# A chunked recurrence in 256 chunks instead of 128, with its states added to the output by accumulating transfers

## The chip, the cores and the metric

The kernel runs on one core of a Trainium2 chip. A core has five engines with a queue of instructions each: TensorE (PE in the profile; PEld is its weight load), VectorE (DVE), ScalarE (ACT), GpSimd (POOL) and SyncE (SP, which here only starts transfers). [...] Sixteen DMA engines move data between the chip's memory (HBM) and the core's two memories: SBUF with 128 partitions, and PSUM, into which TensorE writes. The metric is the device time of one execution in microseconds (us), median of the runs.

## The reference, cut to what matters

The input x has the shape (4, 128, 64, 64): 4 batches, 128 channels, 4096 tokens each. Layer 0 is attention over all tokens of a batch with 64 channels, added to x. Layer 1 takes the tokens, adds causal attention of their normalized form, and then adds a recurrence:

```python
Wx = ((flat - mean) * jax.lax.rsqrt(var + BN_EPS) * gamma + beta).reshape(B, T, H)
def step(yt, wx_t):
    yt = jax.nn.sigmoid(wx_t + yt @ Vt)
    return (yt, yt)
```

`flat` is the normalized token times W, for all batches and tokens; mean and variance are taken over all 16384 rows. `step` runs over the 4096 tokens of a batch, from a state of zeros. The result is the attention result plus the states, for every token. All is float32. V is an orthogonal 128x128 matrix, and the slope of the sigmoid is at most 1/4, so two states that start apart come closer by a factor of four or more with each step.

## The kernel before, in words

The program is `fast_path`, followed by `general_path`, which runs only if `fast_path` has raised a flag. The flag says that a softmax sum left its range or that the cut recurrence did not meet its tolerance.

`fast_path` first does both attention layers, batch after batch, in blocks of 512 query tokens. A loop over items (pairs of key tiles) issues scores (lines 604 and 613), exponentials (618, 620), sums (644, 652) and values (664, 672), with the work of finished blocks slotted in between. The resident tensor `xs` holds x for all batches (64 KB per partition), channels on partitions, and is used over again: after layer 1, `finish1` sends a block's attention result, transposed back, to a scratch tensor `x2` in HBM (line 557), multiplies the normalized tokens by W (563), takes their statistics (564) and copies the product into `xs` (565). At the end of attention, `xs` thus holds Wx for all tokens, and `x2` the attention result.

The tail is the recurrence. It can't be run as 4096 steps in a row, so each batch is cut into `NCH` chunks of `STEPS` tokens, and all chunks of all batches step together: a step is a matmul with as many columns as there are chunks. Before, STEPS is 32 and NCH is 128; 4 batches make 512 columns, in two halves `g` of 256 columns that take turns.

- The attention result is loaded back into `xr` (line 750).
- The normalization's scale and shift are worked out from the statistics (753 to 761), with a square root on ScalarE.
- VectorE makes `wn`, the normalized Wx in step order, in 32 instructions (767).
- A first pass of 32 steps starts all chunks from nothing. Each step preloads `wn` into PSUM with a matmul by the identity (771), adds V times the previous states with a second matmul (782), and takes the sigmoid into SBUF (786). The states of the first 16 steps go to spare tiles, the last of them to `kept`; the later ones replace `wn`.
- The last state of each chunk, shifted by one chunk, is the start of the next (804). A second pass of 16 steps starts from it. Its last states are compared with `kept` (809 to 815): if they agree within 1e-6, the later 16 steps of the first pass stand.
- VectorE adds the states to `xr` in eight instructions, two per batch (833), and SyncE's queue stores the sum (836).
- The counts of both checks meet in `total` (824), one matmul (826) and the flag (827).

The tile library allocates tiles from pools, inserts the semaphore waits, and may move an instruction that is ready ahead of others; each engine's queue then runs in the order built. The helper `normed` has the reciprocal square root of the layer norm: GpSimd's power function (512) and a Newton step of four VectorE instructions (515 to 518).

Of the kernel before, what the change touches and what calls it, by code (L numbers as in the profile page):

```python
# [342 lines left out]
def fast_path(  # L343
# [26 lines left out]
    TPB = BLK // P  # L370
    SHIFT = 32.0
    LOW, HIGH = 1e-25, 1e25
    WARM, TOL, STEPS = 16, 1e-6, 32
    NCH = N // STEPS

    const = ctx.enter_context(tc.tile_pool(name="const", bufs=1))
    xpool = ctx.enter_context(tc.tile_pool(name="x", bufs=1))
    dram = ctx.enter_context(tc.tile_pool(name="dram", bufs=1, space=bass.MemoryType.DRAM))

    xs = xpool.tile([P, B, N], F32, name="xs")

    x2 = dram.tile([B, P, N], F32, name="x2")

    def load(name, shape, *parts):
        t = const.tile(shape, F32, name=name)
# [30 lines left out]
    g1 = const.tile([P, P], F32, name="g1")  # L418
    recs = const.tile([P, 2, B, NT], F32, name="recs")
    stats = const.tile([P, B * NB, nc.vector.BN_STATS_DIM], F32, name="stats")  # L420

    with tc.tile_pool(name="batch", bufs=1) as batch, tc.tile_pool(name="rows", bufs=2) as rowp, tc.tile_pool(
        name="prob", bufs=4
# [78 lines left out]
        def normed(b, g, dst):  # L502

            st = stat.tile([P, TPB, nc.vector.BN_STATS_DIM], F32, tag="st", name="ln_st")
            mv = stat.tile([P, TPB, nc.vector.BN_AGGR_DIM], F32, tag="mv", name="ln_mv")
            for j in range(TPB):
                nc.vector.bn_stats(st[:, j], xs[:, b, ds(g * BLK + j * P, P)])  # L507
                nc.vector.bn_aggr(mv[:, j], st[:, j])
            var = stat.tile([P, TPB], F32, tag="var", name="ln_var")
            nc.vector.tensor_scalar(var, mv[:, :, 1], LN_EPS, None, ALU.add)  # L510
            y = stat.tile([P, TPB], F32, tag="rstd", name="ln_rstd")
            nc.gpsimd.tensor_tensor(y, var, mhalf, ALU.pow)  # L512

            z = stat.tile([P, TPB], F32, tag="z", name="ln_z")
            nc.vector.tensor_tensor(z, y, y, ALU.mult)  # L515
            nc.vector.tensor_tensor(z, z, var, ALU.mult)
            nc.vector.tensor_scalar(z, z, -0.5, 1.5, ALU.mult, ALU.add)
            nc.vector.tensor_tensor(y, y, z, ALU.mult)
# [25 lines left out]
        def finish1(b, g):  # L544
            agg, den = bs[b].agg, bs[b].den
            mem = {}

            def first():
                project(1, b, g, agg, den)
                mem["xh"] = wk.tile([P, TPB, P], F32, tag="xh2", name="xh2")  # L550
                normed(b, g, mem["xh"])

            def second():
                t = xs[:, b, ts(g, BLK)].rearrange("p (j c) -> p j c", c=P)
                xc = wk.tile([P, BLK], F32, tag="xc", name="xc")
# [12 lines left out]
            yield 3, second  # L568
            yield 1, third
# [171 lines left out]

    GB = B // 2
    with tc.tile_pool(name="wn", bufs=1) as wnp, tc.tile_pool(name="y", bufs=2) as yp, tc.tile_pool(
        name="ps_y", bufs=3, space=PSUM
    ) as ps_y:
# [4 lines left out]
        mv = wnp.tile([P, nc.vector.BN_AGGR_DIM], F32, name="mv")  # L752
        nc.vector.bn_aggr(mv, stats)
        scale = wnp.tile([P, 1], F32, name="scale")
        nc.vector.tensor_scalar(scale, mv[:, 1:2], BN_EPS, None, ALU.add)
# [3 lines left out]
        shift = wnp.tile([P, 1], F32, name="shift")  # L759
# [4 lines left out]
        wn = wnp.tile([P, STEPS, B, NCH], F32, name="wn")  # L764
        by_step = xs.rearrange("p b (c s) -> p s b c", s=STEPS)
        for s in range(STEPS):
            nc.vector.tensor_scalar(wn[:, s], by_step[:, s], scale, shift, ALU.mult, ALU.add)

        def preload(s, g):
            ps = ps_y.tile([P, GB, NCH], F32, tag=f"y{g}", name=f"y{g}_ps")  # L770
            nc.tensor.matmul(ps, lhsT=ident, rhs=wn[:, s, ts(g, GB)], start=True, stop=False, skip_group_check=True)  # L771
            return ps

        def run(first, steps, place):

            prev = first
            nxt = [preload(steps[0], g) for g in range(2)]
            for s in steps:
                for g in range(2):
                    ps = nxt[g]  # L780
                    if prev[g] is not None:
                        nc.tensor.matmul(ps, lhsT=vf, rhs=prev[g], start=False, stop=True, skip_group_check=True)  # L782
                    if s != steps[-1]:
                        nxt[g] = preload(s + 1, g)
                    y = place(s, g)
                    nc.scalar.activation(y, ps, AF.Sigmoid)
                    prev[g] = y
            return prev

        kept = [wnp.tile([P, GB, NCH], F32, name=f"kept{g}") for g in range(2)]  # L790

        def place_first(s, g):
            if s == WARM - 1:
                return kept[g]
            if s < WARM:
                return yp.tile([P, GB, NCH], F32, tag=f"y{g}", name=f"y{g}")
            return wn[:, s, ts(g, GB)]

        last = run([None, None], range(STEPS), place_first)

        start = [wnp.tile([P, GB, NCH + 1], F32, name=f"start{g}") for g in range(2)]
        for g in range(2):
            nc.gpsimd.memset(start[g][:, :, 0:1], 0.0)
            nc.vector.tensor_copy(start[g][:, :, 1:], last[g])
        again = run([start[g][:, :, :NCH] for g in range(2)], range(WARM), lambda s, g: wn[:, s, ts(g, GB)])


        for g in range(2):
            nc.vector.tensor_tensor(kept[g], again[g], kept[g], ALU.subtract)
        count = wnp.tile([P, 3], F32, name="count")  # L810
        for g in range(2):
            k = kept[g].rearrange("p b c -> p (b c)")
            nc.vector.tensor_tensor(k, k, k, ALU.mult)
            nc.vector.tensor_scalar(k, k, TOL * TOL, None, ALU.is_le)
            nc.vector.tensor_reduce(count[:, g : g + 1], k, AX.X, ALU.add)

        r = recs.rearrange("p l b t -> p (l b t)")
        r2 = start[0].rearrange("p b c -> p (b c)")[:, : 2 * B * NT]
# [3 lines left out]
        nc.vector.tensor_reduce(count[:, 2:3], r, AX.X, ALU.add)  # L822
        total = wnp.tile([P, 1], F32, name="total")
# [3 lines left out]
        nc.vector.tensor_scalar(flag, tp, P * (B * NCH + 2 * B * NT) - 0.5, None, ALU.is_lt)  # L827

        for b in range(B):
            yb = wn[:, :, b, :]  # L830
            xb = xr[:, b, :].rearrange("p (c s) -> p s c", s=STEPS)
            for part in (slice(WARM, STEPS), slice(0, WARM)):
                nc.vector.tensor_tensor(xb[:, part], xb[:, part], yb[:, part], ALU.add)  # L833
# [61 lines left out]
```

## Time and profile before

The profile is of one execution; its span runs from the first to the last instruction on the core.

| what | value |
|---|---|
| median of 3 runs | 2282.46 us (2281.8 to 2282.84) |
| the profiled execution's own time | 2282.64 us |
| its span | 2280.9 us |
| TensorE matmuls, busy | 2221.0 us, 97% |
| VectorE busy | 1416.9 us, 62% |
| ScalarE busy | 1001.4 us, 44% |
| GpSimd busy | 104.7 us, 5% |
| moved by DMA | 36.17 MB |
| last matmul of attention (line 563) | starts at 2156.7 us |
| first matmul of the recurrence (line 771) | 2163.2 us |
| last sigmoid ends | 2250.6 us |

Positions in time are microseconds from the start of the span. A group's line names the source line, the engine and the operation, what it writes and reads, and the count; then busy time, mean time of one in nanoseconds, and the idle time of the engine before it with what ended it. A line of the timeline has start, duration, engine, line and operation, and in square brackets the idle time before. An instruction's duration contains some latency that the next on the same engine overlaps.

### The profile page before, as it was taken

The numbers are of one execution on the slowest core, as the hardware profiler recorded it, in microseconds if no ns is written. First come the engines' busy times: TensorE is split into PE (matmuls) and PEld (weight loads), VectorE is DVE, ScalarE is ACT, GpSimd is POOL, SyncE is SP. The second block draws the span as 40 slices with busy tenths as digits, with TensorE's granted clock in tenths as the row PEclk, the third lists the DMA queues.
The fourth block names the chain that finished last, engine by engine and source line by source line (L and its number), as shares of the span: only waits on it lengthen the run. The fifth ranks groups of instructions, "written<-read, shape, count | busy, mean of one in ns | idle before, by whom it ended". The sixth has DMA issues, their size and how long they took to land.

```text
span 2280.9 us, 31663 instructions
## 1 busy us (share of the span) xinstructions
PE 2221.0 (97%) x12928; PEld 1043.9 (46%) x12928; DVE 1416.9 (62%) x2607; ACT 1001.4 (44%) x1108; POOL 104.7 (5%) x207
## 2 busy tenths in 40 slices
PE   7999999999999999999999999999999999999894
PEld 3434355454333345544434445554434335554483
DVE  4877764444788764544687875454577786544435
ACT  3666623333566533333566642323466653333242
POOL 0000000000000000000000001000000001000000
PEclk9999999999999999999999999999999999999897
DMA  4000000000000000000000000000000000000123
GB/s 157 1 1 1 1 10 10 5 5 5 6 1 1 1 5 10 10 5 5 6 1 1 1 1 10 10 5 10 5 1 1 1 1 10 10 5 5 65 93 149
DMA packets 10536, 36.17 MB, mean 16 GB/s; under 512 B 1936, under 2 KB 2704, under 8 KB 8848
## 3 DMA queue, kind: packets, MB, share of 16 engines
q1 hardware_dynamic: 8640, 33.56, 3.8%
q8 instruction: 103, 1.69, 0.3%
q10 hardware_dynamic: 1744, 0.53, 0.1%
q14 instruction: 49, 0.40, 0.1%
HBM read 17.30 MB, written 16.78 MB: 15 GB/s over the span
## 4 chain that ended last, share of the span: by engine, by line
PE 95%; DVE 3%; issue 1%; DMA 0%; POOL 0%; ACT 0%; ACTq 0%; POOLq 0%; DVEq 0%
PE s_ps L613 20%; PE acc L672 20%; PE s_ps L604 20%; PE acc L664 19%; PE o_ps L493 3%; PE den_ps L488 2%; PE y_ps L771 2%; PE y_ps L782 2%; PE r_ps L465 1%; PE wx_ps L563 1%; PE v_ps L460 1%; PE r_ps L479 1%; DVE xr L833 1%; PE kc_ps L452 1%; PE xhT_ps L528 1%
## 5 line engine op out<-in xcount | busy, mean ns | idle before, releaser
L644 DVE TENSOR_TENSOR dsum<-dsum,p 128x1024 f32<-128x1024 f32 x676 | 827.7, 1224 | 507.7 <-ACT p L620 336.5
L618 ACT ACTIVATE p<-s_ps,nshift 128x1024 f32<-128x1024 f32 x512 | 571.4, 1116 | 379.7 <-PE s_ps L604 379.2
L620 ACT ACTIVATE p<-s_ps 128x1024 f32<-128x1024 f32 (+2 forms) x288 | 274.5, 953 | 632.4 <-PE s_ps L613 551.5
L604 PE MATMUL s_ps<-rows,kc 64*64 64x512 f32 x4096 | 538.4, 594 | 0.0
L664 PE MATMUL acc<-p,v 64*64 64x512 f32 x4096 | 535.0, 590 | 0.0
L613 PE MATMUL s_ps<-rows,xhT 128*128 128x512 f32 (+3 forms) x1152 | 504.8, 560 | 2.6 <-DVE rows L481 2.6
L672 PE MATMUL acc<-p,xh 128*128 128x512 f32 (+3 forms) x1152 | 501.5, 557 | 0.0
L672 PEld LDWEIGHTS acc<-p,xh 128*128 128x128 f32 x1152 | 215.8, 190 | 243.4 <-issue 234.9
L613 PEld LDWEIGHTS s_ps<-rows,xhT 128*128 128x128 f32 x1152 | 210.4, 190 | 229.1 <-issue 184.6
L664 PEld LDWEIGHTS acc<-p,v 64*64 64x64 f32 x4096 | 158.9, 133 | 279.9 <-issue 273.9
L604 PEld LDWEIGHTS s_ps<-rows,kc 64*64 64x64 f32 x4096 | 146.9, 133 | 248.3 <-issue 233.8
L512 POOL TENSOR_TENSOR ln_rstd<-ln_var,mhalf 128x4 f32<-128x4 f32 x64 | 66.7, 1042 | 1222.9 <-DVE ln_var L510 1212.1
L498 DVE SCALAR_TENSOR_TENSOR xs<-o_ps,recs,xs 128x128 f32<-128x128 f32 x256 | 72.9, 344 | 38.4 <-PE o_ps L493 38.4
L652 DVE TENSOR_TENSOR dsum<-dsum,p 128x256 f32<-128x256 f32 (+1 forms) x120 | 55.9, 496 | 64.3 <-POOL p L624 64.3
L488 PEld LDWEIGHTS den_ps<-ones,den 128*128 128x128 f32 x512 | 64.6, 191 | 40.5 <-issue 20.5
L642 DVE COPY dsum<-p 128x1024 f32<-128x1024 f32 x60 | 41.4, 690 | 61.7 <-ACT p L620 55.4
L520 DVE TENSOR_SCALAR xh<-xs,ln_mv,ln_rstd 128x128 f32<-128x128 f32 x256 | 71.2, 341 | 1.9
L624 POOL TENSOR_SCALAR_AFFINE_SELECT p<-p 128x128 f32<-128x128 f32 x128 | 34.5, 293 | 743.1 <-ACT p L620 743.1
L488 PE MATMUL den_ps<-ones,den 128*128 128x1 f32 x512 | 63.9, 246 | 0.0
L771 PE MATMUL y_ps<-wn,ident 128*128 128x256 f32 x192 | 58.4, 393 | 5.5 <-issue 5.5
L507 DVE BATCH_NORM_STATS2 ln_st<-xs 128x6 f32<-128x128 f32 x256 | 63.4, 269 | 0.0
L515 DVE TENSOR_TENSOR ln_z<-ln_rstd 128x4 f32<-128x4 f32 x64 | 10.4, 163 | 68.7 <-POOL ln_rstd L512 68.7
(94 smaller groups left out, 1140.1 us busy)
## 6 DMA issues: line engine op xcount, KB each, us to landing
xs<-in_x SPq DMA_DIRECT2D x16, 512.0 KB, 9.1
x<-xc SPq DMA_DIRECT2D x32, 256.0 KB, 2.0
xr<-x SPq DMA_DIRECT2D x4, 2048.0 KB, 14.8
out_x<-xr SPq DMA_DIRECT2D x8, 1024.0 KB, 6.0
wk<-in_c_wkT ACTq DMA_DIRECT2D x2, 32.0 KB, 5.0
wo<-in_c_woT ACTq DMA_DIRECT2D x2, 32.0 KB, 4.3
wqT<-in_a_wqT ACTq DMA_DIRECT2D x1, 64.0 KB, 5.0
wkT<-in_a_wkT ACTq DMA_DIRECT2D x1, 64.0 KB, 5.4
```

What stands on the lines that cost most here:

```text
L488: nc.tensor.matmul(dp[:, j : j + 1], lhsT=den[:, ts(j, P)], rhs=ones, start=True, stop=True)
L493: nc.tensor.matmul(op[:, ts(j, P)], lhsT=agg[:, ts(j, P)], rhs=wv1 if layer else wo2, start=True, stop=True)
L498: nc.vector.scalar_tensor_tensor(t, in0=op[:, ts(j, P)], scalar=rec[:, j : j + 1], in1=t, op0=ALU.mult, op1=ALU.add)
L520: nc.vector.tensor_scalar(dst[:, j], xs[:, b, ds(g * BLK + j * P, P)], mv[:, j, 0:1], y[:, j : j + 1], ALU.subtract, ALU.mult)
L604: nc.tensor.matmul(ps[c * M : c * M + M, off : off + n], lhsT=bs[it.b].kc[part, ds(t % (NT // 2) * P + c * M, M)], rhs=rows[part], start=True,
L613: nc.tensor.matmul(ps[:, off : off + n], lhsT=lhsT, rhs=rhs, start=True, stop=True)
L618: nc.scalar.activation(it.p[:, :off], ps[:, :off], AF.Exp, bias=nshift)
L620: nc.scalar.activation(it.p[:, :off], ps[:, :off], AF.Exp, scale=float(P) ** -0.5)
L644: nc.vector.tensor_tensor(flat, flat, it.p, ALU.add)
L664: nc.tensor.matmul(bt.acc[r][h * M : h * M + M], lhsT=bt.v[part, t], rhs=it.p[part, o : o + n], start=it.first, stop=it.last,)
L672: nc.tensor.matmul(bt.acc[0][:, q0:], lhsT=bt.xh[:, t], rhs=it.p[:, o : o + n], start=it.first and h == 0, stop=it.last and h == 1,)
L771: nc.tensor.matmul(ps, lhsT=ident, rhs=wn[:, s, ts(g, GB)], start=True, stop=False, skip_group_check=True)
```

## The change

- The cut is finer: STEPS is 16, so NCH is 256, and a step of one batch alone has 256 columns. The four batches are four separate chains.
- The two passes become one. Each chunk's start is found first, in WARM = 12 steps on the last 12 tokens of the chunk before it (255 columns, since the first chunk starts from zeros); then its own 16 steps run. A batch takes 28 steps. The state at the end of the warm steps is kept in `start` and compared at the end with the last state of the chunk before.
- There is no `wn` and no preload by matmul. A step is one matmul into PSUM, one VectorE instruction that multiplies Wx by the scale and adds it to PSUM in place, and a sigmoid with the shift as its bias. Wx is read from `xs` in place, at a stride of 16 elements, and the states of the 16 own steps are written back into the same places of `xs`.
- The order of the steps of the four batches is fixed by a list `turns`, sorted by step number times a pace per batch, so batch 0 runs ahead and batch 3 ends last.
- `finish1` stores the attention result directly in the output tensor; `x2` and `xr` are gone. When a batch has done its last step, a transfer from GpSimd's queue adds that batch's states to the output in HBM.
- The scale is worked out with the power and Newton step of `normed`, now a helper `rsqrt`, instead of the square root on ScalarE.

```diff
-    WARM, TOL, STEPS = 16, 1e-6, 32
+    WARM, TOL, STEPS = 12, 1e-6, 16
...
+    def rsqrt(y, var, z):
+
+        nc.gpsimd.tensor_tensor(y, var, mhalf[:, : y.shape[-1]], ALU.pow)
+        nc.vector.tensor_tensor(z, y, y, ALU.mult)
+        nc.vector.tensor_tensor(z, z, var, ALU.mult)
+        nc.vector.tensor_scalar(z, z, -0.5, 1.5, ALU.mult, ALU.add)
+        nc.vector.tensor_tensor(y, y, z, ALU.mult)
...
-                nc.sync.dma_start(out=x2[b, :, ts(g, BLK)], in_=xc)
+                nc.sync.dma_start(out=out[b, :, ts(g, BLK)], in_=xc)
...
-        xr = wnp.tile([P, B, N], F32, name="xr")
-        for b in range(B):
-            nc.sync.dma_start(out=xr[:, b], in_=x2[b])
...
-        nc.vector.reciprocal(scale, scale)
-        nc.scalar.activation(scale, scale, AF.Sqrt)
+        rsqrt(scale, var, xrp.tile([P, 1], F32, name="z"))
...
+        by_step = xs.rearrange("p b (c s) -> p b s c", s=STEPS)
+        start = xrp.tile([P, B, NCH], F32, name="start")
+        nc.gpsimd.memset(start[:, :, 0:1], 0.0)
+        prev = [None] * B
+
+        def step(b, s):
+
+            wx = by_step[:, b, s] if s >= 0 else by_step[:, b, STEPS + s, : NCH - 1]
+            n = wx.shape[-1]
+            if s == -1:
+                y = start[:, b, 1:]
+            elif s < 0:
+                y = yp.tile([P, NCH - 1], F32, tag=f"y{b}", name="y")
+            else:
+                y = wx
+            if prev[b] is None:
+                nc.scalar.activation(y, wx, AF.Sigmoid, scale=scale, bias=shift)
+            else:
+                ps = ps_y.tile([P, NCH], F32, tag=f"y{b}", name="y_ps")
+                nc.tensor.matmul(ps[:, :n], lhsT=vf, rhs=prev[b], start=True, stop=True)
+                nc.vector.scalar_tensor_tensor(
+                    ps[:, :n], in0=wx, scalar=scale, in1=ps[:, :n], op0=ALU.mult, op1=ALU.add
+                )
+                nc.scalar.activation(y, ps[:, :n], AF.Sigmoid, bias=shift)
+            prev[b] = start[:, b] if s == -1 else y
+            if s == STEPS - 1:
+                nc.gpsimd.dma_start(out=out[b], in_=xs[:, b], accum_op=ALU.add, max_dma_last_dim=8192)
+
+
+        pace = (1.40, 1.60, 1.75, 1.87)
+        turns = [((s + WARM + 1) * pace[b], b, s) for b in range(B) for s in range(-WARM, STEPS)]
+        for _, b, s in sorted(turns):
+            step(b, s)
...
+        d = xrp.tile([P, B, NCH - 1], F32, name="d")
+        nc.vector.tensor_tensor(d, by_step[:, :, STEPS - 1][:, :, : NCH - 1], start[:, :, 1:], ALU.subtract)
+        nc.vector.tensor_tensor(d, d, d, ALU.mult)
+        nc.vector.tensor_scalar(d, d, TOL * TOL, None, ALU.is_le)
+        nc.vector.tensor_reduce(count[:, 0:1], d.rearrange("p b c -> p (b c)"), AX.X, ALU.add)
...
-        for b in range(B):
-            yb = wn[:, :, b, :]
-            xb = xr[:, b, :].rearrange("p (c s) -> p s c", s=STEPS)
-            for part in (slice(WARM, STEPS), slice(0, WARM)):
-                nc.vector.tensor_tensor(xb[:, part], xb[:, part], yb[:, part], ALU.add)
-            for h in range(2):
-                half = slice(h * N // 2, (h + 1) * N // 2)
-                nc.sync.dma_start(out=out[b, :, half], in_=xr[:, b, half])
```

More of the change, by code (lines that the diff above doesn't have):

```diff
@@ L377, in fast_path @@
     xpool = ctx.enter_context(tc.tile_pool(name="x", bufs=1))
-    dram = ctx.enter_context(tc.tile_pool(name="dram", bufs=1, space=bass.MemoryType.DRAM))
     xs = xpool.tile([P, B, N], F32, name="xs")
-    x2 = dram.tile([B, P, N], F32, name="x2")
     def load(name, shape, *parts):
@@ L511, in normed @@
             y = stat.tile([P, TPB], F32, tag="rstd", name="ln_rstd")
[L512 to L518, printed above, removed]
+            rsqrt(y, var, stat.tile([P, TPB], F32, tag="z", name="ln_z"))
             for j in range(TPB):
@@ L737, in fast_path @@
         assert not waiting and not side
-    GB = B // 2
-    with tc.tile_pool(name="wn", bufs=1) as wnp, tc.tile_pool(name="y", bufs=2) as yp, tc.tile_pool(
-        name="ps_y", bufs=3, space=PSUM
+    with tc.tile_pool(name="xr", bufs=1) as xrp, tc.tile_pool(name="y", bufs=3) as yp, tc.tile_pool(
+        name="ps_y", bufs=2, space=PSUM
     ) as ps_y:
-        xr = wnp.tile([P, B, N], F32, name="xr")
-        for b in range(B):
-            nc.sync.dma_start(out=xr[:, b], in_=x2[b])
-        mv = wnp.tile([P, nc.vector.BN_AGGR_DIM], F32, name="mv")
+        mv = xrp.tile([P, nc.vector.BN_AGGR_DIM], F32, name="mv")
@@ L753, in fast_path @@
         nc.vector.bn_aggr(mv, stats)
-        scale = wnp.tile([P, 1], F32, name="scale")
-        nc.vector.tensor_scalar(scale, mv[:, 1:2], BN_EPS, None, ALU.add)
-        nc.vector.reciprocal(scale, scale)
-        nc.scalar.activation(scale, scale, AF.Sqrt)
+        scale = xrp.tile([P, 1], F32, name="scale")
+        var = xrp.tile([P, 1], F32, name="var")
+        nc.vector.tensor_scalar(var, mv[:, 1:2], BN_EPS, None, ALU.add)
+        rsqrt(scale, var, xrp.tile([P, 1], F32, name="z"))
         nc.vector.tensor_tensor(scale, scale, gamma, ALU.mult)
-        shift = wnp.tile([P, 1], F32, name="shift")
+        shift = xrp.tile([P, 1], F32, name="shift")
@@ L760, in fast_path @@
         nc.vector.tensor_tensor(shift, mv[:, 0:1], scale, ALU.mult)
         nc.vector.tensor_tensor(shift, beta, shift, ALU.subtract)
[L764 to L815, printed above, removed]
+        by_step = xs.rearrange("p b (c s) -> p b s c", s=STEPS)
@@ new lines, in fast_path @@
+        pace = (1.40, 1.60, 1.75, 1.87)
+        turns = [((s + WARM + 1) * pace[b], b, s) for b in range(B) for s in range(-WARM, STEPS)]
+        for _, b, s in sorted(turns):
+            step(b, s)
+        count = xrp.tile([P, 2], F32, name="count")
+        d = xrp.tile([P, B, NCH - 1], F32, name="d")
+        nc.vector.tensor_tensor(d, by_step[:, :, STEPS - 1][:, :, : NCH - 1], start[:, :, 1:], ALU.subtract)
+        nc.vector.tensor_tensor(d, d, d, ALU.mult)
+        nc.vector.tensor_scalar(d, d, TOL * TOL, None, ALU.is_le)
@@ L817, in fast_path @@
+        nc.vector.tensor_reduce(count[:, 0:1], d.rearrange("p b c -> p (b c)"), AX.X, ALU.add)
         r = recs.rearrange("p l b t -> p (l b t)")
-        r2 = start[0].rearrange("p b c -> p (b c)")[:, : 2 * B * NT]
+        r2 = xrp.tile([P, 2 * B * NT], F32, name="r2")
         nc.vector.tensor_scalar(r2, r, LOW, None, ALU.is_ge)
@@ L821, in fast_path @@
         nc.vector.tensor_tensor(r, r, r2, ALU.mult)
-        nc.vector.tensor_reduce(count[:, 2:3], r, AX.X, ALU.add)
-        total = wnp.tile([P, 1], F32, name="total")
+        nc.vector.tensor_reduce(count[:, 1:2], r, AX.X, ALU.add)
+        total = xrp.tile([P, 1], F32, name="total")
         nc.vector.tensor_reduce(total, count, AX.X, ALU.add)
@@ L826, in fast_path @@
         nc.tensor.matmul(tp, lhsT=total, rhs=ones, start=True, stop=True)
-        nc.vector.tensor_scalar(flag, tp, P * (B * NCH + 2 * B * NT) - 0.5, None, ALU.is_lt)
-        for b in range(B):
-            yb = wn[:, :, b, :]
-            xb = xr[:, b, :].rearrange("p (c s) -> p s c", s=STEPS)
-            for part in (slice(WARM, STEPS), slice(0, WARM)):
-                nc.vector.tensor_tensor(xb[:, part], xb[:, part], yb[:, part], ALU.add)
-            for h in range(2):
-                half = slice(h * N // 2, (h + 1) * N // 2)
-                nc.sync.dma_start(out=out[b, :, half], in_=xr[:, b, half])
+        nc.vector.tensor_scalar(flag, tp, P * (B * (NCH - 1) + 2 * B * NT) - 0.5, None, ALU.is_lt)
 def kernel(
```

## The prediction

> **What bounds the kernel now.** I read the page first: the span is 2280.9 us and the profiled run took 2282.64, so 1.74 us lies outside the span; the median of the three runs is 2282.46. The slices by time come next:
>
> ```profile
> PE   7999999999999999999999999999999999999894
> ...
> DVE  4877764444788764544687875454577786544435
> ...
> DMA  4000000000000000000000000000000000000123
> ```
>
> A slice is 57 us. TensorE is full in all but the last, and the transfers stand in the last three. So there are two programs: attention up to about 2157 us, bound by TensorE, and a tail of 123 us. Up to the last block the instructions of attention are the same in both kernels, so only the tail is priced. Its stretches:
>
> ```profile
> 2180.00:2200.00 20.00, 20.00 (x94) 17.61 (x93) 4.50 (x7) 8.93 (x24) 0.00 (x0) 1.00 0.00 1
> ...
> 2240.00:2260.00 20.00, 10.22 (x48) 8.66 (x46) 9.75 (x10) 4.99 (x13) 0.00 (x0) 0.86 0.24 98
> 2260.00:2281.00 21.00, 0.19 (x2) 0.09 (x2) 8.44 (x5) 0.00 (x0) 0.00 (x0) 0.50 0.76 310
> ```
>
> Columns: PE, PEld, DVE, ACT, POOL busy (instructions), PE clock, DMA share, GB/s. In the recurrence PE is busy 20.00 of 20.00 us and ACT 8.93; after 2250 only DVE and DMA work. The groups of the tail, by shape:
>
> ```profile
> L771 PE MATMUL y_ps<-wn,ident 128*128 128x256 f32 x192 | 58.4, 393 | 5.5 <-issue 5.5
> ...
> L782 PE MATMUL y_ps<-wn,vf 128*128 128x256 f32 x120 | 35.0, 379 | 0.0
> L833 DVE TENSOR_TENSOR xr<-xr,wn 128x2048 f32<-128x2048 f32 x8 | 32.7, 4134 | 0.0
> L786 ACT ACTIVATE wn<-y_ps 128x256 f32<-128x256 f32 x64 | 24.6, 384 | 32.1 <-PE y_ps L782 32.0
> ...
> L767 DVE TENSOR_SCALAR wn<-xs,scale,shift 128x512 f32<-128x512 f32 x32 | 22.2, 793 | 0.0
> ```
>
> The chain of waits shows every matmul at 0.43 us (two instructions of 0.215). A step of one half (two batches) is a preload (L771) and a recurrent matmul (L782), 0.86 us. There are (32+16) x 2 = 96 of them: 83 us, all TensorE. Measured: first matmul 2163.2, last sigmoid ends 2250.6, 87.4 us. Then 17.8 us of adds (L833) and about 12 us of transfer.
>
> For the latency of a dependent step I need a place where PE was idle:
>
> ```profile
> 2224.94 0.30 DVE L804 COPY start<-wn 128x256 f32<-128x256 f32 x1
> ...
> 2225.38 0.67 PE L782 MATMUL y_ps<-start,vf 128*128 128x256 f32 x2 [1.68 <-DVE start L804]
> ...
> 2226.09 0.39 ACT L786 ACTIVATE wn<-y_ps 128x256 f32<-128x256 f32 x1 [2.40 <-PE y_ps L782]
> ```
>
> From the end of the operand (2225.24) to the start of the reader (2226.09) a matmul costs 0.85 us at full clock. A sigmoid starts some 0.03 us after a DVE result (L565 after L564).
>
> **What the skill says.** (1) The Trainium skill, "DMA: Bandwidth & Descriptors", section "SWDGE vs HWDGE vs iDMA": accumulating transfers go only from GpSimd, which writes their descriptors in software. The trace has no such transfer. (2) "Collectives: The Full Stack", "The bandwidth ceiling": an add in the DMA engine reads two sources on one ring, so it runs at half the rate of a copy. No run here shows it yet. (3) "Vector Engine (DVE) Microarchitecture Reference", 5.2: a DVE stream that hops at every element takes 1.73 ns a column with one source hopping, 1.98 with all, against 1.05. L833 (source and target strided by 128 B) takes (4.13 - 0.16)/2048 = 1.94 ns: agrees. (4) "ScalarE: Activation LUTs", "What ACT_TABLE_LOAD costs": a pointer operand adds about 93 ns. These two agree (91 ns at 128x1024):
>
> ```profile
> L618 ACT ACTIVATE p<-s_ps,nshift x512: 1114/1115/1121, 29.6 to 1882.9; 128x1024 f32<-128x1024 f32 x171
> ```
> ```profile
> L620 ACT ACTIVATE p<-s_ps x288: 491/1024/1027, 281.6 to 2143.1; 128x1024 f32<-128x1024 f32 x112, 128x896 f32<-128x896 f32 x32
> ```
>
> **The change, part by part.**
>
> *Start of the tail.* Removed: the square root on ACT with its two table loads on the path (DVE result 2159.99, next DVE 2161.67: 1.7 us). Added: GpSimd's power, 1.04 us (L512), and four DVE steps at 0.2 us, 1.9 us with the hand-overs. In the built order the sigmoid's table load stands behind the last copy on ACT with no wait, so its 1.28 us lies beside the statistics. The wn pass also goes, of which the first step (0.9 us) was on the path. The built order also moves the record checks into the last block: one fits DVE's gap at 2147.96 to 2148.82, the reduction hides under the power; two small ones (0.22 + 0.39) are on the path, 0.6 us. Sum: the first sigmoid can start at about 2163.2, where the first matmul starts now.
>
> *Recurrence.* 28 turns for each of 4 batches, 112 in all, each with 255 or 256 columns: matmul, DVE multiply-add in PSUM, sigmoid. PE: 108 x 0.43 = 46 us, no longer full. ACT: 0.384 + 0.093 = 0.48 us, 0.09 of it overlapped when back to back. DVE: the nearest row is L498 (128x128, PSUM, 0.342 us, one every 0.263). 128 more columns at 1.04 would give 0.476; but the source steps by 64 B, so I price 256 at 1.73: 0.65 us, one every 0.57. Bounds: 1.04 (step free) and 2.47 ns (L767, if its two halves run side by side: (782-150)/256). ACT's strided write in the last 16 turns and PE's strided read in the last 15 are unknown; a gain is excluded, since the unstrided form is the base. Upper end: 0.9 ns x 256 = 0.23 us for ACT (DVE's 1.73 against ACT's 0.83), about 0.2 us for PE. I take zero for both.
>
> Chain of one turn: 0.85 + 0.65 + 0.03 + 0.48 = 2.01 us. The order on every engine is fixed by pace: between two turns of batch 0 lie 1.40 x (1/1.40 + 1/1.60 + 1/1.75 + 1/1.87) = 3.42 turns, of DVE 3.42 x 0.57 = 1.95 us. The two nearly meet: 2.05 us a turn with a little jostling. Batch 0: 27 x 2.05 = 55.4, first sigmoid from SBUF 0.6, and four cold microseconds of PE (clock 0.50 until 2168) about 3: 60 us after 2163.2. The other batches keep their share (27 turns at 1.87/1.40 of the time at worst, less once batches drop out): the last at about 75 us. Before this took 87.4.
>
> *Output.* The 32 writes of the attention result keep their size, queue and place and only change their target: nothing, under attention's matmuls. Removed: the 8 MB reload (hidden then; DMA was idle otherwise) and eight adds of 4.1 us, four of which (17.8 us with small ops) stood on the path. Added: four accumulating transfers of 2.10 MB on GpSimd's queue. Each waits for its batch's last sigmoid; nothing else is queued behind them on GpSimd but the flag's load, which is needed at the end. Copies here ran at 410 to 425 GB/s; half is 212 GB/s: 9.9 us each. The four follow one another: 60 + 1 (descriptors) + 39.6. The last batch is ready at 75, its transfer's turn comes at 60 + 1 + 29.7 = 90.7, so the batches' later ends are hidden; if they weren't, each us of theirs would count. Landing and end of program: before, data stopped about 2278.5 and the span ended 2280.9; I allow 2 + 2 us. The check on the states (6 to 7 us of DVE after 75) is hidden under the transfers.
>
> *Sum.* 2163.2 + 60 + 1 + 39.6 + 4 = 2267.8 of span, against 2280.9; plus 1.7: 2269.5.
>
> **Rivals.**
> 1. *Slow accumulation (slower).* The transfers become the bound in earnest: half rate is a rule from elsewhere. If reads and the write share an engine's time (a third of the rate), a transfer takes 14.8 us and the four 59: 2289. It decides from 14.2 us each, where the 39.6 grow by the 13 us gained plus 4.6. For it: software descriptors, 8 KB pieces, no trace. Against: source and target lie in different memories.
> 2. *Strided operands (about even).* DVE at 2.47 ns: 3.42 x 0.76 = 2.6 us a turn, batch 0 at 75, total 2284.5. With DVE at 1.73 and both other strides at the upper end: 16 x 0.2 + 15 x 0.2 = 6, total 2276. For it: L767 and L833 both pay for stride. Against: only one stream of three is strided here, at half the step.
> 3. *Accumulation at copy rate.* 4.9 us each: the last batch sets the end: 2163.2 + 75 + 1 + 4.9 + 4 + 1.7 = 2250.
> 4. *The change does not do what it says.* If the seam check fails with 12 steps ahead, the general path runs as well and the time grows by far more than the range. A slope of at most 1/4 and an orthogonal matrix make 4^-12 = 6e-8 of the start error, below the tolerance of 1e-6.
>
> **How the numbers follow.** My forecast (2260 to 2278) gets 0.53, rival 2 beyond that 0.16, rival 1 0.19, rival 3 0.10, rival 4 0.02. The predicted time is the forecast's, 2269.5. 8 in 10: leaving out most of rival 3 and the far end of rival 1, 2256 to 2291. A measurement tells 0.2% (4.6 us): faster below 2277.9: 0.53 + 0.10 + 0.08 of rival 2 = 0.71; within: 0.08; slower, above 2287: 0.21.
>
> **What would show it.** The multiply-add at about 0.65 us (0.48: stride free; over 0.8: rival 2); the sigmoid into the states' tensor at 0.48 or more; batch 0's transfer issued about 60 us after the first sigmoid; PE no longer full in the tail; landings 10 us apart, with DMA's share near one between them (15 apart: rival 1, 5: rival 3); the chain of waits ending in DMA, not DVE. I am wrong if PE's clock falls back to 0.50 in the recurrence (0.43 more a turn, which adds 27 x 0.4 = 11 us to batch 0), or if a transfer waits for its forerunner's landing.

## The result: slower by 6 us, with the output still waiting at the end

| | before | after |
|---|---|---|
| median | 2282.56 us (2281.8 to 2282.84, 4 runs) | 2288.89 us (2288.21 to 2289.95, 4 runs) |
| span of the profiled execution | 2280.9 us | 2287.0 us |
| first instruction of the recurrence | 2163.2 us | 2160.8 us |
| last sigmoid ends | 2250.6 us | 2243.2 us |
| from there to the end of the span | 30.3 us | 43.8 us |

The ratio after to before is 1.0029, with a 95% interval of 1.0011 to 1.0046. The prediction was 2269.5 us, a gain of 13 us. The time lies inside the predicted range, near its upper end, and on the wrong side of the time before.

The tail of the changed kernel by stretches of 10 us, in the columns used before (PE, PEld, DVE, ACT, POOL busy, PE clock, DMA share, GB/s):

```profile
2180.00:2190.00 10.00, 9.90 (x37) 5.26 (x36) 10.00 (x20) 8.67 (x19) 0.00 (x0) 1.00 0.00 0
2190.00:2200.00 10.00, 10.00 (x24) 4.82 (x24) 7.85 (x13) 8.45 (x13) 0.00 (x0) 1.00 0.00 0
2200.00:2210.00 10.00, 10.00 (x24) 4.75 (x23) 7.81 (x13) 8.31 (x13) 0.00 (x0) 1.00 0.00 0
...
2240.00:2250.00 10.00, 2.00 (x7) 0.62 (x5) 7.36 (x9) 2.87 (x4) 5.04 (x4) 0.73 0.74 135
2250.00:2260.00 10.00, 0.00 (x0) 0.00 (x0) 0.00 (x0) 0.00 (x0) 0.00 (x0) 0.50 1.05 216
...
2270.00:2280.00 10.00, 0.00 (x0) 0.00 (x0) 0.00 (x0) 0.00 (x0) 0.00 (x0) 0.50 1.05 218
```

Two things stand in these rows that the prediction did not have. Until 2190 VectorE is full, as foreseen. Then the own steps begin, VectorE falls to 7.8 of 10 us, and TensorE runs only 24 instructions in 10 us instead of 37. (Its busy column is near 10 in both stages and can't tell them apart; the waits below do.) And DMA moves next to nothing until the recurrence is over: from 2250 on no engine works, and the transfers run alone at 210 to 218 GB/s.

The groups of the tail by shape (name, shape, count, then busy time, mean duration in ns, and idle time before with what ended it):

```profile
L777 PE MATMUL y_ps<-xs,vf 128*128 128x256 f32 x120 | 52.0, 608 | 0.1
L781 ACT ACTIVATE xs<-y_ps,shift 128x256 f32<-128x256 f32 x64 | 45.7, 722 | 8.5 <-DVE y_ps L778 2.7
L778 DVE SCALAR_TENSOR_TENSOR y_ps<-xs,scale,y_ps 128x256 f32<-128x256 f32 x64 | 43.2, 682 | 11.0 <-PE y_ps L777 11.0
L777 PE MATMUL y_ps<-y,vf 128*128 128x255 f32 x88 | 25.8, 450 | 4.9 <-ACT y L774 4.9
...
L777 PEld LDWEIGHTS y_ps<-xs,vf 128*128 128x128 f32 x120 | 24.6, 206 | 27.1 <-issue 26.3 <-ACT xs L781 0.8
L781 ACT ACTIVATE y<-y_ps,shift 128x255 f32<-128x255 f32 x40 | 18.9, 473 | 4.2 <-DVE y_ps L778 1.4
...
L784 POOL DMA_DIRECT2D out_x<-xs x4 | 5.0, 1937 | 81.6 <-ACT xs L781 81.6
```

The same two lines of code appear twice each. With a contiguous operand (`y`) a sigmoid takes 473 ns. Writing its states into `xs` at a step of 64 bytes, it takes 722. A matmul is two instructions, which took 0.43 us together in the kernel before; the one that reads `xs` fills TensorE for 52.0 us in 60 turns, 0.87 us a turn. Its weight loads (PEld) show that TensorE itself is the bound there: of their 27.1 us of idle time, 26.3 are "issue", in which nothing else was waited for. VectorE's instruction reads `xs` at the same step in both stages and hardly differs. The chain of waits agrees on who sets the pace, first VectorE (warm steps), then TensorE (own steps); each line has start, duration, engine, tile and count:

```profile
2166.25 22.75 DVE y_ps L778 x41
2189.80 52.03 PE y_ps L777 x120
2243.26 1.88 DVE d L795
```

The last group of the tail above says that GpSimd sat idle for 81.6 us until a sigmoid let the first transfer go. The instructions on the output tensor (durations, then first and last start):

```profile
L784 POOL DMA_DIRECT2D out_x<-xs x4: 1360/1913/2562, 2241.1 to 2243.5; - x4
```

All four transfers are issued within 2.4 us of one another. The batches did not finish one after the other: they ended together, and all 40 us of transfers stand behind them. The chain above says the same: its 120 matmul instructions on `xs` from 2189.80 on are all there are, in one row, so no batch had begun its matmuls on own states while another was in its warm steps. The durations account for the date: 12 warm steps of 4 x 0.57 us and 16 own steps of 4 x 0.87 make 83 us, and from the first sigmoid to the last end 82.4 were measured.

### The profile page after: what moved, and what is told of

It is laid out like the page before. It is cut to its first block, busy times and chain, and to the rows that moved or that the text cites. A ratio compares the mean times of both kernels' runs of the same rounds, so it can differ in the third digit from the quotient of the medians.

```text
span 2287.0 us, 31380 instructions
## 1 busy us (share of the span) xinstructions
PE 2214.5 (97%) x12764; PEld 1010.5 (44%) x12764; DVE 1433.6 (63%) x2672; ACT 1032.0 (45%) x1122; POOL 110.6 (5%) x211
## 4 chain that ended last, share of the span: by engine, by line
PE 94%; DVE 3%; issue 1%; DMA 0%; POOL 0%; ACT 0%; ACTq 0%; DVEq 0%; POOLq 0%
PE s_ps L612 20%; PE acc L671 20%; PE s_ps L603 19%; PE acc L663 19%; PE o_ps L498 3%; PE y_ps L777 2%; PE den_ps L493 2%; PE r_ps L470 1%; PE v_ps L465 1%; PE wx_ps L562 1%; PE r_ps L484 1%; DVE y_ps L778 1%; PE xhT_ps L527 1%; PE kc_ps L457 1%; PE xT_ps L479 1%; PE xh2T_ps L527 1%
## 5 line engine op out<-in xcount | busy, mean ns | idle before, releaser
L778 DVE SCALAR_TENSOR_TENSOR y_ps<-xs,scale,y_ps 128x256 f32<-128x256 f32 (+1 forms) x108 | 67.9, 676 | 13.8 <-PE y_ps L777 13.7
L493 PE MATMUL den_ps<-ones,den 128*128 128x1 f32 x512 | 63.9, 246 | 0.0
```

The lines of the kernel that those rows point to most:

```text
L493: nc.tensor.matmul(dp[:, j : j + 1], lhsT=den[:, ts(j, P)], rhs=ones, start=True, stop=True)
L778: nc.vector.scalar_tensor_tensor(ps[:, :n], in0=wx, scalar=scale, in1=ps[:, :n], op0=ALU.mult, op1=ALU.add)
```

## The experiments

**Theory A** after this reading: two things, each worth several microseconds, ate the gain. (1) The four batches run in step, turn by turn, instead of at the four paces of the list `turns`, so no transfer overlaps the recurrence. (2) TensorE and ScalarE pay for the 64-byte step of `xs`. **A rival (B)**: the order is not at fault, since an engine that is full takes the same total time in any order; or the transfers, once they start earlier, only run slower beside the recurrence. **A second rival**: the accumulation itself is what costs, whatever the order.

All results, each beside the kernel before on the same chip (2281.76 us for the first four, 2281.51 for the last three; the changed kernel wasn't run again on those chips, so differences of spans to it, given below, are good to about 1 us, by which the kernel before differs between the chips; attention, unchanged, ends at slightly different times too, so that the first sigmoid stands at 2160.8 in the changed kernel and at 2161.4 to 2162.4 in the first four runs). By the medians the first three runs lie 6.6, 16.4 and 19.2 us below the changed kernel; by the spans of the profiled executions, used below, 7.3, 15.6 and 19.3:

| run | what is different from the changed kernel | median us | ratio to before, 95% interval | span |
|---|---|---|---|---|
| e1_paced | order of the list kept | 2282.29 | 1.0002 (0.9993 to 1.0011) | 2279.7 |
| e2_contig | own states contiguous, GpSimd copies them | 2272.49 | 0.9960 (0.9946 to 0.9974) | 2271.4 |
| e3_paced_contig | both | 2269.72 | 0.9950 (0.9933 to 0.9966) | 2267.7 |
| e4_plain_store | plain stores, attention result left out | 2269.68 | 0.9948 (0.9928 to 0.9967) | 2267.6 |
| e5_reload_add | output as before the change | 2275.86 | 0.9975 (0.9964 to 0.9985) | 2274.1 |
| e6_blocked | e3, and Wx in step order by blocks | 2262.56 | 0.9916 (0.9900 to 0.9933) | 2260.6 |
| e7_blocked_add | e6, GpSimd adds, plain stores | 2256.98 | 0.9890 (0.9874 to 0.9907) | 2255.6 |

### The order of the list kept (e1_paced)

Each matmul, multiply-add and sigmoid of `step` is marked to stay in the order in which the program lists it. No operand and no wait is changed.

```diff
+        pin = tc.keep_in_program_order
...
-                nc.tensor.matmul(ps[:, :n], lhsT=vf, rhs=prev[b], start=True, stop=True)
+                pin(nc.tensor.matmul(ps[:, :n], lhsT=vf, rhs=prev[b], start=True, stop=True))
```

> The changed kernel with each matmul, multiply-add and sigmoid of the recurrence pinned behind the one written before it on its engine, so that the order of the list turns is the order built (the changed kernel's built order goes round 0, 1, 2, 3). Theory A, the order is what failed: with the durations of the changed kernel's profile (PE 0.86 us a turn in the own steps, DVE one every 0.57, chain 2.0 to 2.9) batch 0 ends about 2232, the last batch about 2253, the first transfer starts about 2233 beside the recurrence, and four transfers of 9.9 us end the span at about 2279: 2281 us, 8 below the changed kernel. Rival B, transfers from GpSimd can't run beside the recurrence (descriptors held up, or each waits for all states): they still start after the last sigmoid, then at about 2253, and the time is about 2299. Rival C, only the strides matter: no gain, 2287 to 2291.

Measured: 2282.29 us, span 2279.7, which is 7.3 us below the changed kernel's. The instructions on the output tensor, and a stretch of the tail:

```profile
L785 POOL DMA_DIRECT2D out_x<-xs x4: 1178/1195/1360, 2234.1 to 2255.3; - x4
```

```profile
2240.00:2250.00 10.00, 7.50 (x16) 3.77 (x16) 5.30 (x8) 5.84 (x9) 1.19 (x1) 0.58 1.03 202
```

Batch 0's transfer now goes 7 us earlier and the last one 12 us later, and between 2240 and 2250 DMA is full at 202 GB/s while the matmuls go on. With VectorE's 0.57 and TensorE's 0.87 us a turn and 3.42 turns between two of batch 0, 12 x 1.95 + 16 x 2.98 = 71 us are due to its end; 72.6 were measured from the first sigmoid (2161.5). So the recurrence as a whole became longer (last issue 2255.3 against 2243.5; towards the end, with two batches left and then one, a batch's own latency of 2.7 us a turn sets the pace) and the kernel faster: the sum is set by when the *first* batch ends, plus four transfers in a row. The rival falls in both of its forms: neither was the time the same, nor did the transfers run slower beside the recurrence (202 to 214 GB/s). The order alone brings the kernel back to the time of before and no further.

### Own states contiguous (e2_contig)

The sigmoid of an own step writes a contiguous tile `w`, which the next matmul reads; GpSimd, idle otherwise, copies it into its strided place. The order is that of the changed kernel.

```diff
-                y = wx
+                y = yp.tile([P, NCH], F32, tag=f"w{b}", name="w")
...
+            if s >= 0:
+                nc.gpsimd.tensor_copy(wx, y)
```

> The changed kernel, but the own steps' sigmoid writes a contiguous tile, which the next matmul reads, and GpSimd copies it into its strided place in the states' tensor (64 copies of 128x256 added on an engine that is idle). Order as built before, round 0, 1, 2, 3. Theory of the strides: PE falls from 0.86 to 0.43 us a turn and the sigmoid from 0.72 to 0.47 in the own steps; DVE at 0.57 every turn is then the bound, the last sigmoid comes at about 2225 instead of 2243, the span ends at about 2270: 2271.5 us. Theory A alone: the ends still fall together, so the 40 us of transfers stay exposed, and whatever the recurrence gains shows in full. If strides cost nothing beyond what hides behind DVE: 2287 to 2291. If GpSimd's strided copies are slower than 1.1 us each they become the bound (64 x 1.1 = 70 us from about 2187): over 2300.

Measured: 2272.49 us, span 2271.4, 15.6 us below the changed kernel. The groups of its tail:

```profile
L784 POOL COPY xs<-w 128x256 f32<-128x256 f32 x64 | 37.6, 659 | 30.5 <-ACT w L781 30.5
L778 DVE SCALAR_TENSOR_TENSOR y_ps<-xs,scale,y_ps 128x256 f32<-128x256 f32 x64 | 36.2, 683 | 0.0
L777 PE MATMUL y_ps<-w,vf 128*128 128x256 f32 x120 | 34.0, 431 | 0.0
L781 ACT ACTIVATE w<-y_ps,shift 128x256 f32<-128x256 f32 x64 | 30.4, 475 | 5.7 <-POOL xs L784 0.2
```

The matmul's instruction falls from 608 to 431 ns and the sigmoid from 722 to 475. The weight loads now wait for the sigmoid, so TensorE has time to spare:

```profile
L777 PEld LDWEIGHTS y_ps<-w,vf 128*128 128x128 f32 x120 | 17.8, 188 | 16.0 <-ACT w L781 16.0
```

VectorE, at 683 ns as ever, has no idle time left: it is a bound now, with one multiply-add in every 0.57 us (36.2 over 64). The strided writes did not vanish, they moved to an engine that had nothing to do. GpSimd keeps up with VectorE, but only just: between 2200 and 2220 it too is busy for all of the time, and its last copies end some 5 us after VectorE's last multiply-add, the issue of transfers between them. The run mends both strides at once; that TensorE's made the gain is read from these waits, not from a run of its own.

### Both (e3_paced_contig)

> Both edits: order pinned, and own steps contiguous with GpSimd copying. Batch 0 ends about 2219, the last about 2235, and four transfers of 9.9 us follow from 2221: span about 2266, 2268 us. If the two gains simply added (8 + 17 below 2288.9) it would be 2264; if GpSimd's queue, which now has copies and the transfers' issues (1.4 to 2.6 us each) in one line, holds up either, 2270 or more.

Measured: 2269.72 us, span 2267.7. This is the kernel that the prediction had in mind, in order and in operands: 2267.8 of span and 2269.5 us were predicted. That the spans agree to 0.1 us is in part luck, for the first sigmoid starts 1.8 us earlier than predicted, at 2161.4, batch 0's transfer is issued 60.9 us later (60 predicted), and the rest takes 45.4 us instead of 44.6:

```profile
L787 POOL DMA_DIRECT2D out_x<-xs x4: 1178/1195/1367, 2222.3 to 2238.0; - x4
```

The two causes are not additive: 7.3 and 15.6 us alone, 19.3 together. In round-robin order the contiguous states already bring all batches' ends, the first one's too, forward: the first transfer is issued at 2226.3, 63.9 us after the first sigmoid. The order takes 3 us more off that.

### Plain stores (e4_plain_store)

The transfers of the changed kernel go out as plain stores on SyncE's queue. The addition of the attention result is left out; the output holds the states alone.

```diff
-                nc.gpsimd.dma_start(out=out[b], in_=xs[:, b], accum_op=ALU.add, max_dma_last_dim=8192)
+                nc.sync.dma_start(out=out[b], in_=xs[:, b])
```

> The changed kernel with a plain store from SyncE's queue in place of the accumulating transfer. It leaves out the addition of the attention result: the output holds the states alone. Theory: the accumulating transfer's price is its two reads; a plain store of 2.10 MB takes 5.0 us, the four 20, and the span ends at about 2243 + 20 + 4 = 2267: 2269 us. If the price is in the strip of descriptors or the HBM and not in the addition, the four still take 30 to 40 us and the time stays above 2279.

Measured: 2269.68 us, span 2267.6. The recurrence is unchanged. One stretch beside the changed kernel's row for the same time (216 GB/s, above):

```profile
2250.00:2260.00 10.00, 0.19 (x2) 0.09 (x2) 0.30 (x2) 0.00 (x0) 0.00 (x0) 0.50 1.02 419
```

The same bytes at 419 instead of 216 GB/s, and 19.4 us less: an accumulating transfer costs twice a plain one. The edit changes the queue along with it (SyncE's for GpSimd's), so the price of the addition by itself is not shown; DMA's share is full in both rows. So the second rival holds in part: the accumulating output is 20 us dearer than plain stores. But the prediction had priced it so; it is no part of the miss.

### The output of before on the new recurrence (e5_reload_add)

The attention result goes to a scratch tensor again, is loaded back into `xr`, and VectorE adds.

```diff
+        xr = xrp.tile([P, B, N], F32, name="xr")
+        for b in range(B):
+            nc.sync.dma_start(out=xr[:, b], in_=x2[b])
...
-                nc.gpsimd.dma_start(out=out[b], in_=xs[:, b], accum_op=ALU.add, max_dma_last_dim=8192)
+                for h in range(2):
+                    half = slice(h * N // 2, (h + 1) * N // 2)
+                    nc.vector.tensor_tensor(xr[:, b, half], xr[:, b, half], xs[:, b, half], ALU.add)
+                    nc.sync.dma_start(out=out[b, :, half], in_=xr[:, b, half])
```

> The recurrence of the changed kernel, untouched, with the output of the kernel before: the attention result goes to a scratch tensor, is loaded back before the recurrence, VectorE adds the states in eight contiguous instructions, SyncE stores with plain transfers. Theory (the accumulating transfers cost 40 us in a row at the end, and the order of the steps exposes all of it): the recurrence ends as in the changed kernel, 2241 to 2243 us; the adds are contiguous now, 2048 columns at 1.05 ns + 0.16 = 2.3 us each, 18.4 in all, with the stores (2.5 us a half) beside them; last store lands about 2264, span 2266 to 2272, that is 15 to 21 us below the changed kernel. Rival (the old output is as dear as it was, 4.1 us an add, 33 in all): span about 2281 to 2285.

Measured: 2275.86 us, span 2274.1: 12.9 us below the changed kernel, and 2 us above the upper end of what was expected. The group of the adds, and below it the timeline of VectorE's last work:

```profile
L791 DVE TENSOR_TENSOR xr<-xr,xs 128x2048 f32<-128x2048 f32 x8 | 17.8, 2302 | 0.8 <-ACT xs L786 0.8
```

```profile
2258.20 4.49 DVE L791 TENSOR_TENSOR xr<-xr,xs 128x2048 f32<-128x2048 f32 x2 [0.75 <-ACT xs L786]
...
2262.61 1.86 DVE L803 TENSOR_TENSOR d<-xs,start 128x1020 f32<-128x1020 f32 x1
...
2268.17 0.15 DVE L818 TENSOR_SCALAR flag<-tp 1x1 int32<-1x1 f32 x1 [0.28 <-PE tp L817]
```

An add takes 2.30 us, not 4.13 as in the kernel before, because the states now lie in token order in `xs`. The expectation had left out three things that the trace shows. The check on the states, which lies beside the transfers in the changed kernel, stands behind the adds on VectorE (2262.6 to 2268.3), and the flag follows. The first sigmoid starts 2.3 us later than in the changed kernel (2163.1), because in this built order ScalarE's table load (1.28 us) stands behind the shift and not beside the statistics. And VectorE's last multiply-add (2256.8) stands behind six of the adds, so that VectorE waits 0.75 us for the last sigmoid. Which of these makes the 2 us is not shown; no run took one away. So on this recurrence the accumulating output was not needed to lose the old adds' price, and it is the dearer of the two ways.

### Wx in step order by blocks (e6_blocked)

With contiguous states VectorE was a bound in e2. Here `finish1` leaves Wx of a block of 512 tokens in step order, so that a step reads runs of 32 contiguous elements; the copies of the states go to a token-ordered tile `yt`, from which the accumulating transfers read. Warm steps take 256 columns, with the last one unused. Order and contiguous states as in e3.

```diff
-                nc.scalar.copy(xs[:, b, ts(g, BLK)], wp)
+                nc.scalar.copy(
+                    xs[:, b, ts(g, BLK)].rearrange("p (s c) -> p s c", s=STEPS), wp.rearrange("p (c s) -> p s c", s=STEPS)
+                )
...
-        by_step = xs.rearrange("p b (c s) -> p b s c", s=STEPS)
+        by_step = xs.rearrange("p b (g s c) -> p b s g c", g=NB, s=STEPS)
+        yt = xrp.tile([P, B, N], F32, name="yt")
+        by_token = yt.rearrange("p b (c s) -> p b s c", s=STEPS)
...
+                nc.gpsimd.tensor_copy(by_token[:, b, s], y)
```

> On top of the fixed order and the contiguous states: finish1 leaves Wx of each block of 512 tokens in step order (runs of 32 contiguous elements), warm steps take 256 columns, and GpSimd copies each step's states into a token-ordered tile, from which the accumulating transfers go. Theory (VectorE's multiply-add pays for its 64-byte step, and after the other two strides it is the bound): the multiply-add falls from 0.68 to about 0.48 us, one every 0.40; TensorE at 0.43 a turn becomes the bound; batch 0 is done about 2217, four transfers of 9.9 us follow, span 2255 to 2260. Rival (runs of 32 cost as much as a full stride, or VectorE isn't the bound): span as with fixed order and contiguous states, 2266 to 2269.

Measured: 2262.56 us, span 2260.6, 7.1 below e3. Two groups of its tail:

```profile
L784 DVE SCALAR_TENSOR_TENSOR y_ps<-xs,scale,y_ps 128x256 f32<-128x256 f32 x108 | 49.0, 489 | 17.9 <-PE y_ps L783 17.2
...
L790 POOL COPY yt<-y 128x256 f32<-128x256 f32 x60 | 32.1, 727 | 32.7 <-ACT y L787 32.7
```

The multiply-add takes 489 ns (480 expected), 0.19 us less than at the full stride, and VectorE now waits for TensorE (17.2 us). The span is 0.6 us above the upper end of what was expected; as in e5 the table load stands behind the shift, and the first sigmoid starts at 2163.0, 1.6 us later than in e3. The first transfer is issued at 2215.7 and four in a row set the end.

### The same, with GpSimd adding and plain stores (e7_blocked_add)

```diff
-                nc.gpsimd.tensor_copy(by_token[:, b, s], y)
+                nc.gpsimd.tensor_tensor(by_token[:, b, s], by_token[:, b, s], y, ALU.add)
...
-                nc.gpsimd.dma_start(out=out[b], in_=yt[:, b], accum_op=ALU.add, max_dma_last_dim=8192)
+                nc.sync.dma_start(out=out[b], in_=xr[:, b])
```

`by_token` is now a view of `xr`, into which the attention result is loaded beside the warm steps.

> As the one before, but the attention result is loaded back before the recurrence and GpSimd adds each step's states into it, so that plain stores from SyncE's queue (5 us a batch) end the kernel. Theory (with the accumulation at half rate gone and the strides gone, the end is set by the last batch's last step): if GpSimd's strided add takes what its strided copy took (0.62 us), 64 of them are 40 us and keep up; last step about 2230, span 2238 to 2246. Rival (a strided add on GpSimd reads a second strided operand and takes about 1.0 us): 64 us from about 2190 make GpSimd the bound, span 2258 to 2264.

Measured: 2256.98 us, span 2255.6, the fastest of all: 1.1% below the kernel before (interval 0.9% to 1.3%). The group of the adds and, after it, a stretch of the tail:

```profile
L795 POOL TENSOR_TENSOR xr<-xr,y 128x256 f32<-128x256 f32 x60 | 50.3, 1046 | 29.6 <-ACT y L792 29.5
```

```profile
2220.00:2230.00 10.00, 6.38 (x16) 3.60 (x15) 3.71 (x8) 4.02 (x9) 10.00 (x14) 0.68 0.17 73
```

The theory's 2238 to 2246 was too short by 9.6 us or more. The rival's mechanism holds, and its time was 2 to 8 us too long: an add reports 1.05 us, of which back-to-back ones overlap a part (one every 0.84, from 50.3 over 60), and GpSimd is full from about 2200 on. The accumulation's half rate is gone, and the next bound is GpSimd. Sharing its adds with VectorE wasn't tried.

## Why the prediction was wrong, step by step

**The step that failed** is in the part "Recurrence": "*The order on every engine is fixed by pace: between two turns of batch 0 lie ... 3.42 turns*". The list `turns` fixes the order in which the program *names* the steps. As the front of this document says, the tile library may move an instruction that is ready ahead of others, and it did: the four batches end within 2.4 us of one another. From that step came "60 us after 2163.2" for batch 0 (its parts, 55.4 + 0.6 + 3, make 59.0) and so an overlap of transfers with the recurrence that did not exist. Kept in the list's order (e1), the span falls by 7.3 us. On the first transfer's date the prediction's chain 2163.2 + 60 reads 2160.8 + 80.3 as measured: 2.4 us earlier in its start, 20.3 later in its length. The rest, from that issue to the end of the span, is 45.9 us against 44.6. The three differences make up the 19.2 us by which the span was missed. Of the 20.3, the order takes off 7.7 (72.6 us from the first sigmoid to the first issue in e1) and contiguous states then 11.7 more (60.9 in e3).

**A term was mis-sized** in the same part, and it is the larger of the two causes: "*I take zero for both*", of ScalarE's strided write and TensorE's strided read. They measured 0.25 us a sigmoid (722 against 473 ns; the upper end was 0.23) and 0.43 us a matmul (0.87 against 0.43; the upper end was 0.2). The price of the second is no small addition but a doubling, so TensorE became the bound of the own steps. The prediction's upper end (16 x 0.2 + 15 x 0.2 = 6 us) also charged each stride once a turn of batch 0, though the turns of the other batches, 3.42 in all, go through the same TensorE; the measured 11.7 us are the price with the order kept. Contiguous operands alone (e2) save 15.6 us and would have made the kernel faster than before; the order alone (e1) only brings it even. The upper end for ScalarE was made by carrying over VectorE's price per column, and it nearly held; TensorE's was set without any row for it, and it did not. The Trainium skill, "SBUF — State Buffer", section "Door 1: The DMA port swizzle", says that each access which crosses to a new 16-byte line pays a penalty, so that four fp32 elements is how far one can step for free. A step of 16 elements crosses a line every time, and the trace's prices an element are 0.76 ns for VectorE ((683 - 489)/256, against runs of 32 in e6), 0.97 ns for ScalarE ((722 - 473)/256) and 1.7 ns for TensorE ((0.87 - 0.43) us/256). By that section all three had to pay, and all three do; the prediction charged one.

What held:

- *Start of the tail*, to 2.4 us: first sigmoid predicted at 2163.2, measured 2160.8. The power took 0.55 us instead of 1.04, and the last block came 1.3 us earlier (its `o_ps` matmuls at 2146.3 against 2147.6), which is drift of attention and luck. The table load (2158.2, beside the statistics) cost nothing; the two small record checks stand on the chain with 0.18 and 0.37 us, about as predicted.
- *VectorE's multiply-add*: 0.65 us and one every 0.57 predicted; 0.68 and 0.57 measured. The stride is dear by what the Trainium skill says, "Vector Engine (DVE) Microarchitecture Reference", 5.2 (1.73 ns a column with one source hopping, a row measured at a much larger hop than the 64 bytes here), and rival 2's 2.47 ns a column is refuted. Runs of 32 (e6) bring 0.49.
- *Sigmoid on contiguous operands*: 0.48 predicted, 0.473 measured.
- *Accumulating transfer*: 9.9 us each predicted from half the copy rate; four took about 40 at 210 to 218 GB/s. Rivals 1 and 3 are refuted. The rule that the prediction took from the Trainium skill, "Collectives: The Full Stack", "The bandwidth ceiling", that an add in the DMA engine reads two sources and so runs at half rate, agrees with this trace: 216 against 419 GB/s in e4, which changes the queue too.
- *The seam check* holds with 12 steps ahead, so rival 4 did not occur. The clock is 1.00 from 2170 to 2240 in the changed kernel. It does fall in other runs, late, where TensorE waits: to 0.50 after 2242 in e1 and after 2224 in e7, where a matmul then takes 1.22 us instead of 0.71; in e7 GpSimd was the bound by then.

**Rival 2**, strided operands, was the right mechanism at the wrong engine: it made VectorE's stride dear and the other two cheap, and ended about even. The outcome on the slower side came from two causes that met: the stride's price on TensorE, and the transfers that lost their cover. The prediction let everything hang on batch 0's early end, and built no rival on the batches ending together.

The prediction's own signs would have told it apart at once: "batch 0's transfer issued about 60 us after the first sigmoid" (80 measured) and "PE no longer full in the tail" (the bound from 2190 on).

## What to carry to other kernels

An order that a loop or a sorted list suggests is not the order that is built: where overlap depends on who finishes first, look at the order of the built queues, or at the spread of the issue times, before pricing anything. When a change makes an existing tensor the operand of other engines in place, each engine's stride has its own price; an operand that is read by a matmul should be contiguous, and the strided move should go to an engine that is idle. And a transfer at the end costs its full time unless the first piece of data is ready early: four equal pieces that become ready together overlap with nothing.

## What the runs showed of the hardware that was not expected

- TensorE reading fp32 columns 64 bytes apart takes 0.87 us for 128x256 instead of 0.43, twice as long. ScalarE writing at this step takes 0.72 instead of 0.47.
- GpSimd does the strided copy of 256 columns in 0.66 to 0.73 us with no slowdown of VectorE's multiply-add (683 ns in e2, 682 without), of which only one operand lies in SBUF.
- In e7 a VectorE subtraction with both operands in SBUF did not get through beside GpSimd's adds. Its timeline, with the next instruction:

```profile
2236.94 6.54 DVE L808 TENSOR_TENSOR d<-last,start 128x1020 f32<-128x1020 f32 x1 [0.54 <-ACT last L792]
...
2243.51 1.22 DVE L809 TENSOR_TENSOR d<-d 128x1020 f32<-128x1020 f32 x1
```

In e6 the same instruction took 1.22 us, and there it was GpSimd's copy, begun 0.04 us after it, that took 1.66 us instead of the 0.62 of the one before. In e7 GpSimd's last add ended at 2242.4; 2242.4 + 1.1 is the end of this one. The Trainium skill, "SBUF — State Buffer", "Who interferes with whom", has it that a VectorE instruction with two SBUF inputs and a GpSimd instruction that reads SBUF exclude one another, and that one with at most one SBUF input doesn't contend. Both sentences agree with these runs; but the wait in e7, as the timeline reads, lasted until GpSimd's whole row of queued adds was done, not one of them.
